# Spreading an image's prologue over the image before it, with the depthwise convolution on TensorE and per-token factors in the epilogue

## The chip, the cores and the metric

One Trainium2 chip (trn2), one core. The metric is the device time of one execution in microseconds (us), the median of several runs. Engines are named as the profile names them: PE is TensorE, PEld its weight loads, DVE is VectorE, ACT ScalarE, POOL GpSimd, SP the engine in whose queue nearly all DMAs are issued.

## The reference, cut to what matters

Four images of 48 × 48 tokens with 128 channels go through layer 0 (a group norm, a projection, a 3 × 3 depthwise convolution, a selective scan in four directions, a gated layer norm and a projection), then through attention and a spectral layer, which the change leaves alone.

```python
xz = einsum('bhwc,ec->bhwe', _gn(x), in_proj_w)          # 128 -> 2 * 256
xin, z = split(xz, 2, axis=-1)
xc = silu(depthwise_3x3(xin, conv_w) + conv_b)           # B, 256, 48, 48
xs = stack([x0, x1, x0[..., ::-1], x1[..., ::-1]])       # rows, columns, both reversed; L = 2304
# ... dt = softplus(...), B_t and C_t by projections of xs
def step(h, inp):                                        # h: B, 4, 256, 16
    dt_l, u_l, B_l, C_l = inp
    h = h * exp(dt_l[..., None] * A) + (dt_l * u_l)[..., None] * B_l[:, :, None, :]
    return h, einsum('bkdn,bkn->bkd', h, C_l)
# ... y: the four directions added, tokens by 256
y = (y - mu) * rsqrt(var + 1e-05) * norm_g + norm_b
x = x + einsum('bhwd,cd->bhwc', y * silu(z), out_proj_w)
```

## The kernel before

Each image is worked through in 20 chunks (five per direction: four of 480 tokens, one of 384). A chunk is eight *units* (two halves of the 256 channels by four groups of states). A unit makes a product with B, two scans on VectorE, a product with C on GpSimd and a sum over states on TensorE. The *prologue* (norm, projection, convolution, z) of the next image runs at the end of an image, as the first part of the preparation of its first chunk; the *epilogue* (layer norm, gate, projection) follows the last chunk.

```python
    def prologue2(b):
        # ... projection into xpad, SUB = 384 tokens at a time
            nc.vector.tensor_scalar(x, xpad[:, 0:H, 0:W], cw[:, h, 0:1], cb[:, h:h + 1], ALU.mult, ALU.add)
            for t in range(1, 9):
                yield
                dy, dx = divmod(t, 3)
                nc.vector.scalar_tensor_tensor(x, xpad[:, dy:dy + H, dx:dx + W], cw[:, h, t:t + 1], x,
                                               ALU.mult, ALU.add)
            nc.scalar.activation(x, x, AF.Silu)
        # ... z, its SiLU, and its way to DRAM
```

What every chunk sends through SP's queue: B and C (`bcd`) to DRAM early in its preparation; in the fifth unit dt and dt·u (`dtdud`) to DRAM and back, replicated (`rep`); and `fetch`, the broadcasts of rows of `bcd`, which are issued by `multiply` in the last four units of the chunk before.

```python
        def prep(self):
            # ... softplus; then for each half h:
                nc.sync.dma_start(d[h, :, :, :n].rearrange("s p t -> p s t"), re[:, h, :, :n])
                rep = rp.tile([P, 2, G4, CS], F32, tag="rep", name=f"rep{name}_{h}")
                for c in range(C4):
                    nc.sync.dma_start(rep[c * DL:(c + 1) * DL, :, :, :n],
                                      d[h, :, :, :n].rearrange("s (g p) t -> p s g t", p=DL))

        def fetch(self, i):
            t = one.tile([P, CS], F32, tag=f"bc{i}", name=f"bc{self.name}_{i}")
            for c in range(C4):
                nc.sync.dma_start(t[c * DL:(c + 1) * DL, :self.n],
                                  self.bcd[4 * i + c, :self.n].partition_broadcast(DL))

    POOLED = ((0, 3), (1, 1), (1, 3))        # units whose product with B is GpSimd's

    def multiply(s):
        u = units[s]
        u.times_c()
        # ...
        if u.h == NH - 1 and ci < len(chunks):
            chunks[ci].fetch(Q4 + u.q)
            if any(u.q == q for h, q in POOLED):
                chunks[ci].fetch(u.q)
```

The epilogue's core, with full-width factors on VectorE:

```python
        def gate(i):
            rs = rss[:, i % 2]               # 128 x 384, the same in every partition
            nc.vector.reciprocal(rs, rs)
            for h in range(NH):
                v = yf[h][:, cols(i)]
                nc.vector.scalar_tensor_tensor(v, v, ng[:, h:h + 1], rs, ALU.mult, ALU.mult)
                nc.vector.scalar_tensor_tensor(v, v, nb[:, h:h + 1], zr[i][:, h], ALU.add, ALU.mult)
```

## Time and profile before

| | before |
|---|---|
| median of 3 runs | 8763.95 us (8758.15 to 8770.22) |
| profiled execution | 8775.2 us, mean granted clock 0.799 |
| PE, DVE, ACT, POOL busy | 6433.5, 4656.9, 2975.0, 3486.1 us |
| layer 0 | to about 5059 us |
| image to image | 1265.3 us |
| last image, from its third bcd write | 1078.0 us |

The shares of busy time are averages over layer 0 (VectorE and GpSimd full, TensorE a half) and the rest (TensorE alone), so they bound nothing by themselves. The useful ruler is a mark that occurs once per chunk: the DMA that writes `bcd`. The time from one to the next is the length of a chunk, and from an image's third to the next image's third is an image. I count from the third because the writes of an image's first two chunks are mixed with the turn. The prediction below shows the lines of the page, the stretches, the groups and the queue.

### The profile page before, as it was taken

What the parts mean: (1) busy time and instruction counts of PE and PEld (TensorE: products, weight loads), DVE (VectorE), ACT (ScalarE), POOL (GpSimd) and SP (SyncE); (2) the same over time, 40 slices, a digit from 0 to 9 for tenths busy, and PEclk for the clock granted to TensorE, in tenths of its full rate; (3) what the DMA queues carried; (4) which work ended last, traced back from release to release, by engine and by line L of the source; (5) the groups of instructions that cost most, each with busy time, mean ns of one, the idle gap of its engine ahead of it and who ended that gap; (6) DMA issues with size and microseconds to landing.
All of it is one profiled execution on the core that took longest, in us unless ns stands there. A gap on an engine that the chain in (4) does not pass through costs nothing.

```text
span 8775.2 us, 62894 instructions
## 1 busy us (share of the span) xinstructions
PE 6433.5 (73%) x22344; PEld 3227.0 (37%) x22344; DVE 4656.9 (53%) x3905; ACT 2975.0 (34%) x6001; POOL 3486.1 (40%) x936
## 2 busy tenths in 40 slices
PE   4555636655545655455556589899999999999999
PEld 1111112111112111121111145466666666666666
DVE  5888858888768888668888720221111111111111
ACT  3555534555434555435555444400000000000000
POOL 3787735787736777538787600100000000000000
PEclk6666656666666666666666699999999999999999
DMA  3555514555524555425555400000000000000000
GB/s 80 117 120 119 118 49 110 115 121 121 118 57 103 116 120 119 97 65 112 118 120 120 102 25 0 6 5 11 13 8 8 8 8 14 10 8 6 6 6 22
DMA packets 377310, 570.98 MB, mean 65 GB/s; under 512 B 50073, under 2 KB 372761, under 8 KB 376994
## 3 DMA queue, kind: packets, MB, share of 16 engines
q1 hardware_dynamic: 374016, 566.19, 28.1%
q8 instruction: 175, 2.87, 0.1%
q14 instruction: 141, 1.16, 0.0%
q10 hardware_dynamic: 2978, 0.77, 0.0%
HBM read 467.68 MB, written 99.09 MB: 65 GB/s over the span
## 4 chain that ended last, share of the span: by engine, by line
PE 48%; DMA 14%; DVE 12%; issue 6%; POOL 6%; SPq 5%; ACT 3%; POOLq 0%; DVEq 0%; ACTq 0%
PE cv L780 28%; PE pr L793 6%; DMA dtdud<-re 6%; DMA rep<-dtdud 6%; DVE s L372 5%; POOL s L381 4%; PE sp L313 4%; SPq L332 4%; PE s L605 3%; PE o L611 3%; DVE xc L221 2%; DMA bc<-bcd 2%; PE y L390 2%; DVE s L357 2%; ACT dA L365 1%
## 5 line engine op out<-in xcount | busy, mean ns | idle before, releaser
L372 DVE TENSOR_TENSOR_SCAN s<-dA,s 128x962 f32<-128x962 f32 (+1 forms) x1536 | 2590.9, 1744 | 334.6 <-ACT s L369 334.5
L381 POOL TENSOR_TENSOR s<-s,bc 128x1920 f32<-128x1920 f32 (+1 forms) x640 | 2423.5, 3811 | 607.0 <-ACT carry L379 443.9
L780 PE MATMUL cv<-tt,u 128*128 128x384 f32 (+2 forms) x9216 | 2505.5, 433 | 0.0
L390 PE MATMUL y<-s,csum 128*32 128x480 f32 (+1 forms) x5120 | 923.2, 817 | 1546.1 <-POOL s L381 1544.0
L780 PEld LDWEIGHTS cv<-tt,u 128*128 128x128 f32 x9216 | 1648.5, 190 | 869.9
L365 ACT ACTIVATE dA<-rep,A 128x480 f32<-128x480 f32 (+1 forms) x2560 | 1659.2, 648 | 560.3 <-DVE s L372 515.4
L786 DVE COPY U<-cv 128x384 f32<-128x384 f32 x384 | 214.2, 558 | 2244.9 <-PE cv L780 2244.9
L357 POOL TENSOR_TENSOR s<-rep,bc 128x1920 f32<-128x1920 f32 (+1 forms) x240 | 993.6, 4140 | 930.8 <-DMA bc<-bcd 923.1
L784 ACT COPY U<-cv 128x384 f32<-128x384 f32 x384 | 183.6, 478 | 2797.3 <-PE cv L780 2797.3
L761 POOL TENSOR_TENSOR ms<-mp,mm 128x512 f32<-128x512 f32 x16 | 20.3, 1268 | 2717.5 <-DVE G L710 2439.5
L390 PEld LDWEIGHTS y<-s,csum 128*32 128x32 f32 x5120 | 128.2, 130 | 2211.5 <-POOL s L381 1959.0
L357 DVE TENSOR_TENSOR s<-rep,B 128x1920 f32<-128x1920 f32 (+1 forms) x400 | 824.0, 2060 | 35.8 <-PE B L348 17.0
L348 PE MATMUL B<-xd,spread 32*128 32x480 f32 (+1 forms) x800 | 587.1, 824 | 136.3 <-DVE s L357 123.5
L793 PE MATMUL pr<-U,G 128*128 128x288 f32 (+1 forms) x2560 | 519.2, 358 | 0.0
L793 PEld LDWEIGHTS pr<-U,G 128*128 128x128 f32 x2560 | 407.5, 190 | 67.2
L313 PE MATMUL sp<-re,ident 128*128 128x480 f32 (+1 forms) x640 | 391.0, 699 | 18.8 <-ACT re L301 12.4
L319 DVE TENSOR_TENSOR re<-sp,xc 128x480 f32<-128x480 f32 (+1 forms) x160 | 125.8, 786 | 463.8 <-ACT re L316 463.8
L796 DVE TENSOR_TENSOR acc<-acc,pr 128x288 f32<-128x288 f32 x512 | 232.5, 454 | 245.2 <-PE pr L793 245.2
L348 PEld LDWEIGHTS B<-xd,spread 32*128 32x128 f32 x800 | 161.9, 251 | 501.0 <-DVE s L357 250.5
L316 ACT COPY re<-sp 128x480 f32<-128x480 f32 (+1 forms) x160 | 86.7, 542 | 733.1 <-PE sp L313 733.1
L606 ACT ACTIVATE e<-s,shift 128x512 f32<-128x512 f32 (+1 forms) x360 | 230.6, 642 | 290.7 <-PE s L605 273.8
L611 PE MATMUL o<-e,xn 128*128 128x512 f32 (+1 forms) x720 | 293.2, 550 | 0.0
(151 smaller groups left out, 4306.8 us busy)
## 6 DMA issues: line engine op xcount, KB each, us to landing
rep<-dtdud SPq DMA_DIRECT2D x512, 480.0 KB, 8.2
bc<-bcd SPq DMA_DIRECT2D x1536, 60.0 KB, 2.1
dtdud<-re SPq DMA_DIRECT2D x128, 480.0 KB, 9.7
rep<-dtdud SPq DMA_DIRECT2D x128, 384.0 KB, 6.1
tt<-in_phi SPq DMA_DIRECT2D x32, 576.5 KB, 3.7
bc<-bcd SPq DMA_DIRECT2D x384, 48.0 KB, 2.0
dtdud<-re SPq DMA_DIRECT2D x32, 384.0 KB, 3.0
zd<-z SPq DMA_DIRECT2D x24, 384.0 KB, 2.4
```

The source lines that it names most:

```text
L313: nc.tensor.matmul(ps[:, :n], w, t, start=(i == 0), stop=(i == 3))
L332: nc.sync.dma_start(t[c * DL:(c + 1) * DL, :self.n], self.bcd[4 * i + c, :self.n].partition_broadcast(DL))
L348: nc.tensor.matmul(ps[:, :n], spread[32:64, self.q].rearrange("p c j -> p (c j)"), self.ch.xd[32:64, :n], start=True, stop=True)
L357: eng.tensor_tensor(ch.blocks(s)[:, :, ch.cols], ch.rep[self.h][:, 1, :, :n], bt[:, :n].unsqueeze(1).to_broadcast([P, G4, n]), ALU.mult)
L365: nc.scalar.activation(ch.blocks(dA[j], 2)[:, i, ch.cols], ch.rep[self.h][:, 0, g, :n], AF.Exp, scale=A[:, ch.k, self.h * G4 + g, self.q:s ...
L372: nc.vector.tensor_tensor_scan(s, dA[j][:, run], s, 0.0, ALU.mult, ALU.add)
L381: nc.gpsimd.tensor_tensor(s, s, ch.bc[Q4 + self.q][:, :n].unsqueeze(1).to_broadcast([P, G4, n]), ALU.mult)
L390: nc.tensor.matmul(ch.y[g * DL:(g + 1) * DL, :n], csum, s[:, g], start=(self.q == 0), stop=(self.q == Q4 - 1))
L605: nc.tensor.matmul(ps[:, :w], xnT[:, i * P:(i + 1) * P], xnT[:, lo:lo + w], start=True, stop=True)
L611: nc.tensor.matmul(po[q][:, :w], xn[:, i // 2, i % 2, :], e[:, lo:lo + w], start=(i == 0), stop=(i == NT - 1))
L780: nc.tensor.matmul(ps[:, lo - c0:CONV], u[b][:, J, g, :], taps(tt[q], lo - J * P - back, c0 + CONV - J * P - back), start=(J == 0), stop=( ...
L793: nc.tensor.matmul(ps[:, lo - lo0:hi - lo0], G[q][:, s, :], U[q][:, lo:hi], start=(q == 0), stop=(q == 1))
```

## The change

The intent: take the turn between images off the path. The next image's prologue becomes a list of 43 small tasks, of which a chunk takes two or three (in its units 0, 1 and 5, counted from 0; for these tasks the prediction calls unit 5 the fifth) beside its own work. The convolution becomes nine accumulating TensorE matmuls with diagonal weights, over ten rows at a time. SiLU of z moves into the epilogue. There the variance is laid out with tokens on partitions, so that its inverse root is one factor per token, applied after the projection. The convolution's result is held for two images at once, and chunks become 384 tokens long, 24 per image; I take the second to make room for the first. The core, with cuts:

```diff
-CS = 480
+CS = 384
+RB = 10
+    taps = wp.tile([P, NH, 9, P], F32, name="taps")
+    for h in range(NH):
+        for t in range(9):
+            nc.vector.tensor_scalar_mul(taps[:, h, t], ident, cw[:, h, t:t + 1])
 ...
+        def transposed(lo, n, i):
+            x = two.tile([P, 4, C], F32, tag="tok", name=f"x{b}_{i}")
+            nc.sync.dma_start(x[:m, :parts], xs[b][lo:lo + n].rearrange("(i p) c -> p i c", p=m))
+            ps = now["ps"] = mm_tile(f"tr{b}_{i}")
+            for t in range(parts):
+                nc.tensor.transpose(ps[:, t * m:(t + 1) * m], x[:m, t], ident[:m, :m])
+
+        def stats(i):
+            def pe():
+                transposed(i * SUB, SUB, f"s{i}")
+            def rest():                       # emitted one unit later
+                nc.vector.bn_stats(st[:, i], now["ps"][:, :SUB])
 ...
+                        for t in ts:          # taps 0-3 in one unit, 4-8 in the next
+                            dy, dx = divmod(t, 3)
+                            nc.tensor.matmul(out, taps[:, h, t], xpad[h][:, top + dy:top + dy + m, dx:dx + W],
+                                             start=(t == 0), stop=(t == 8))
 ...
+        def variance(i):
+            for t in range(tb):
+                for h in range(NH):
+                    nc.tensor.matmul(var[:, i * tb + t:i * tb + t + 1], sq[i][:, h, t * P:(t + 1) * P],
+                                     dmean[:, 0:1], start=(h == 0), stop=(h == NH - 1))
 ...
+        def fetch(i):
+            zr[i] = two.tile([P, NH, SUB], F32, tag="z", name=f"zr{b}_{i}")
+            nc.sync.dma_start(zr[i], zs[b][:, :, cols(i)].rearrange("h p t -> p h t"))
+            xr[i] = two.tile([P, tb, C], F32, tag="xr", name=f"xr{b}_{i}")
+            nc.sync.dma_start(xr[i], xs[b][cols(i)].rearrange("(t p) c -> p t c", p=P))
         def gate(i):
-            nc.vector.reciprocal(rs, rs)
+            nc.scalar.activation(zr[i], zr[i], AF.Silu)
 ...
+                nc.vector.scalar_tensor_tensor(xr[i][:, t], ps[:, :C], rd[:, i * tb + t:i * tb + t + 1], xr[i][:, t],
+                                               ALU.mult, ALU.add)
 ...
+        fetch(0)
+        for i in range(nblk + 1):
             if i < nblk:
-                center(i)
+                gate(i)
+            if i > 0:
+                project(i - 1)
+            if i + 1 < nblk:
+                fetch(i + 1)
 ...
+        if rest:
+            task = rest
+        elif tasks and (j == 0 or j in (1, 5) and tasks[0][0] == 1):
+            task = tasks.pop(0)
+        if task:
+            begin(task)
```

## The prediction

> **What bounds the kernel now.** I read four views in this order: the page's slices (where the stages lie), the busy time by stretches (the turn between two images against the steady part), the timeline of the DMA-issuing queue (SP), and the chain of waits. From the page:
>
> ```profile
> DVE  5888858888768888668888720221111111111111
> POOL 3787735787736777538787600100000000000000
> PEclk6666656666666666666666699999999999999999
> ```
>
> Each digit is a fortieth of 8775 us, 219 us. Layer 0, the only part that the change touches, is the first 23 slices (to about 5060 us). Attention and the spectral layer after it (3,700 us) stay as they are. In layer 0 VectorE is at 0.8, with three dips to 5 and 6: the turns from one image to the next. TensorE's granted clock is 0.6 there and 0.9 later. Two stretches show a turn against steady work:
>
> ```profile
> 800.00:1090.00 290.00, 172.94 (x540) 44.95 (x539) 247.56 (x155) 161.28 (x318) 233.40 (x62) 0.67 0.56 122
> 1090.00:1354.00 264.00, 108.83 (x284) 34.83 (x284) 163.06 (x82) 88.60 (x154) 102.34 (x24) 0.59 0.28 68
> ```
>
> The columns are TensorE, weight load, VectorE, ScalarE and GpSimd busy us, clock, DMA share, GB/s. In the turn GpSimd falls from 233 of 290 us to 102 of 264 and the DMA share halves: the scan, which feeds both, is held back. What holds it is in the groups of instructions:
>
> ```profile
> L221 DVE SCALAR_TENSOR_TENSOR xc<-xpad,cw,xc 128x2304 f32<-128x2304 f32 x64 | 213.9, 3342 | 1.8
> L429 DVE RECIPROCAL room<-room 128x384 f32<-128x384 f32 x24 | 61.1, 2546 | 0.0
> ```
>
> The first is the depthwise convolution: 8 big instructions per half image, 53 us per image (median 2.6 us, up to 6.5 when it shares time with GpSimd), queued ahead of scans. The second is the epilogue's full-width reciprocal, 15 us per image.
>
> The steady part is not bound by a full engine but by a ring of waits that closes once per chunk. The queue's timeline shows it for a chunk of 480 and then the chunk of 384 that ends each direction:
>
> ```profile
> 544.81 0.38 SPq L321 DMA_DIRECT2D dtdud<-re  x1
> 556.17 1.78 SPq L324 DMA_DIRECT2D rep<-dtdud  x4
> 558.05 2.05 SPq L332 DMA_DIRECT2D bc<-bcd  x4
> 561.45 0.30 SPq L289 DMA_DIRECT2D bcd<-xd  x1
> 563.88 12.82 SPq L332 DMA_DIRECT2D bc<-bcd  x20
> ...
> 598.93 0.38 SPq L321 DMA_DIRECT2D dtdud<-re  x1
> 606.87 1.78 SPq L324 DMA_DIRECT2D rep<-dtdud  x4
> 610.62 1.71 SPq L332 DMA_DIRECT2D bc<-bcd  x4
> 612.42 0.36 SPq L289 DMA_DIRECT2D bcd<-xd  x1
> 614.51 11.32 SPq L332 DMA_DIRECT2D bc<-bcd  x20
> 640.65 0.38 SPq L321 DMA_DIRECT2D dtdud<-re  x1
> ...
> 645.31 0.38 SPq L321 DMA_DIRECT2D dtdud<-re  x1
> ```
>
> Columns: start, time, queue and line, what is moved. The ring: dt and dt·u of the next chunk go to DRAM (L321), come back replicated (L324), then 24 row broadcasts (L332) follow in the same queue; the last of them frees GpSimd, whose product releases a scan, a sum on TensorE, the softplus matmuls, and so the next L321. **First part** (L321 to the last broadcast): 544.81 to 576.70 = 31.9 us with 480, 598.93 to 625.83 = 26.9 with 384. **Second part** (to the next L321): 576.70 to 598.93 = 22.2 with 480; 625.83 to 645.31 = 19.5 with 384. Sum: 54.1 against 46.4 us. So 0.8 of the tokens cost 0.86 of the time: 24 broadcasts have a fixed issue cost. The two 384-chunks that follow one another in the middle of an image confirm it: L289 to L289 is 45.8 us there.
>
> **What the Trainium skill says.** *TensorE: Matmul & The Clock Gate*, Part 1, says that the array runs at half clock after an idle window of about 3.4 us and at full clock after a busy one. The trace agrees: the same eight sums (L390) take 1.83 us after an idle stretch and 1.01 us in a dense one. So convolution matmuls of 480 columns are 0.40 us per pass warm and 0.80 cold (spacing of the weight loads of L313, two passes per matmul). *ScalarE: Activation LUTs*, What ACT_TABLE_LOAD costs, gives 1283 ns per switch of the function set plus a drain; the trace has 1283 ns each (L168, L223, L425). *Perfetto Trace Analysis*, DMA Instruction — HWDGE, says that the profiled window of a DMA instruction leaves out the data movement; the trace agrees (L321 shows 0.38 us, its reader starts 11 us later), so I took gaps in the queue, not durations.
>
> **The change part by part.**
>
> *Size of the turn before.* The third bcd write of image 0 is at 184.9 us, of image 1 at 1450.5: a period of 1265.7 us. The 17 intervals from 184.9 to 1085.4 average 53.0, so 20 chunks are 1060 us and the turn costs 206 us: the epilogue's 55 (1356 to 1411) and 150 of prologue.
>
> *Removed from VectorE:* 8 × 2.6 and 1.5 us, twice per image, with contention 56 us, plus group-norm scaling of 1.5 us. Removed too: ScalarE waiting for it, and the serial ip and z matmuls (each ~8 us).
>
> *Moved to TensorE:* 10 convolutions (5 blocks of rows by 2 halves) of 18 instructions per image, 18 × 0.4 = 7.3 us warm, up to 14.5 cold; 73 to 145 us per image. They are issued in the first two units of a chunk, where TensorE waits 16 to 17 us per chunk for GpSimd (L390 at 586.73 sat 16.1 us idle). They mostly fit, and may warm the array for the sums after them. Hence the 150 us should leave the path.
>
> *Cost of spreading, per image.* 43 tasks in 18 of the chunks. Ten z writes and three token loads fall in the queue's critical part (fifth unit): about 1.5 us each for issue and transfer. Transposes waiting for their tokens at the head of TensorE's queue: 3 × 4 us in that slot. The SiLU with two table loads, 2 × 2.1 + 2 × 1.3 = 6.8 us on ScalarE, mostly exposed. Sum about 37 us; less about 1.2 us for each of 10 chunks with a warm array: 25 us.
>
> *Chunks of 384:* 24 × 46.4 = 1114 us instead of 1060: +54 per image.
>
> *Epilogue.* Gone: reciprocal 15 us, one of two scalar_tensor_tensor (7.8 us), sqrt over full width. Added: the variance as 72 instructions with one column (weight-load bound), and 180 projection instructions instead of 72. L441 issues 14 in 3.37 us, 0.24 each; if warm, 0.15 to 0.19 (otr L630: 18 in 2.6). So projection 27 to 43 us, variance 11 to 17, mean 24 × 0.4 = 10, table loads, filling and draining about 10: 68 us, bound by TensorE instead of VectorE, against 55.
>
> *New period:* 1114 + 68 + 5 (flush, start of y) + 25 = 1212, against 1266: −54, three times = −161. The last image has no next one: +54 body, +13 epilogue. *Start:* the first prologue is now all serial: statistics to about 22 us as before, then 5 blocks of about 22 us (20 of TensorE work, 2 of gaps; the last shorter) = 110, SiLU 7, preparation 31: first scan input at 170 instead of 135.7: +34 us.
>
> **Sum:** −161 + 54 + 13 + 34 = −60; 8764 − 60 = **8704**, say 8705 us.
>
> **Rivals.**
> 1. *The turn vanishes almost freely and the ring gets shorter:* warm TensorE cuts sums and softplus matmuls in every chunk, the epilogue overlaps the queue's 27 us wait. For it: the idle 16 us; VectorE is only 81% needed in a 46 us chunk (37.4 us of work, estimated from 16 scans of 1.66, 5 products of 1.65 and four small ones). Then spreading costs 0 and the epilogue 50: about −190 us, 8575. Against it: in the ring's first part VectorE is busy without a gap, so postponed scans are not free.
> 2. *The spread work lengthens the ring:* evacuations, z writes and transposes that wait for DMA sit in in-order queues, and two PSUM buffers are shared by B, dt, softplus and tasks. For it: the ring has only 2.4 us of slack at VectorE (scan at 583.08). With 3 us in each of 18 chunks, or a cold convolution spilling over the softplus matmuls: spreading 55 to 80, total +30 to +105, about 8830.
> 3. *The turn was hidden anyway.* Against it: GpSimd and DMA halve there, so no.
> 4. *Smaller chunks cost nothing* (24 × 44): −115 more. Against it: the measured 45.8 to 46.4.
>
> **Range and chances.** Spreading 0 to 60 us (times three), epilogue 50 to 85 (times four), start +20 to +90 (cold array): about ±100 us together. 8600 to 8810. Faster by 2% needs 175 us, nearly all of rival 1: 0.16. Slower by 2% needs rival 2 and a cold start: 0.04. Within 2%: 0.80.
>
> **What would show it.** L289 to L289 at 46 to 48 us in chunks with tasks, 46.4 in the last six; no dip of GpSimd at a turn beyond some 75 us; period about 1212; first scan near 170 us; TensorE busy in layer 0 up, its clock somewhat higher; epilogue with TensorE as the dense engine. The prediction is wrong if 384-chunks without tasks differ from 46.4, if chunks with a convolution are over 50 us, or if the epilogue is over 90.

## The result, and the profile after

The changed kernel is correct and took **8839.38 us** (median of 4 runs, 8826.48 to 8843.20) against 8764.69 in the same rounds. The ratio is 1.0083, 95% interval 1.0065 to 1.0100: within 2%, as given the largest chance, but slower where 60 us less was predicted, and outside the range. A ratio here and below is the mean time of one kernel's fast runs over the mean of the other's of the same rounds, so not quite the ratio of the medians quoted.

The slices of the page after, in the same form as those of before; a slice is now 221 us:

```profile
DVE  1777776777876778767788621131111111111111
POOL 1677774677765777757777600000000000000000
PEclk8677767677776777676666689999999999999999
```

VectorE's dips to 5 at the turns are gone, and TensorE's clock in layer 0 is mostly 0.7 instead of 0.6. But the flat level is 7, where it was 8 between the turns. TensorE is busy for 6937.9 us instead of 6433.5 and VectorE for 4390.1 instead of 4656.9. So the work moved as intended, and the plateau between the turns lost what the turns gained. The first slice has fallen from 5 to 1: the start is longer.

The chunks, measured from `bcd` write to `bcd` write:

| | predicted | measured |
|---|---|---|
| image to image (third bcd write to third bcd write) | 1212 | 1243 (1245.3, 1242.1, 1241.3) |
| the first three chunks that carry tasks, per image | | 55.9, 61.5, 57.8 (mean 58.3) |
| the next 15 with tasks | 46 to 48 | 48.2 |
| the last five of the image | 46.4 | 47.1 |
| chunks of the last image, no tasks | 46.4 | 46.9 |
| across the turn, with one chunk in it | 46.4 + 68 + 5 | 111 |
| third bcd write of image 0 | 219 (185 + 34) | 233.3 |

Three stretches, in the columns that the prediction explained: one of the first three chunks with its neighbour's start, one later chunk with tasks, one chunk without:

```profile
284.00:350.00 66.00, 30.99 (x105) 10.72 (x105) 47.30 (x33) 25.28 (x56) 39.18 (x14) 0.60 0.39 89
455.00:504.00 49.00, 38.20 (x127) 12.74 (x119) 38.80 (x26) 27.69 (x57) 36.95 (x12) 0.74 0.50 114
4010.00:4056.00 46.00, 26.67 (x98) 8.57 (x96) 35.47 (x24) 25.30 (x58) 34.24 (x11) 0.65 0.46 108
```

The second stretch has 11.5 us more TensorE work than the third, and such a chunk is only 1.3 us longer (48.2 against 46.9): matmuls between the waits cost little. In the first, TensorE does least for its length (31 of 66 us) and its clock is lowest: it is not overfull but waiting. SP's queue shows for what:

```profile
286.69 1.78 SPq L411 DMA_DIRECT2D bc<-bcd  x4
289.25 0.30 SPq L368 DMA_DIRECT2D bcd<-xd  x1
291.00 0.39 SPq L204 DMA_DIRECT2D x_s<-in_x  x1
293.06 19.18 SPq L411 DMA_DIRECT2D bc<-bcd  x20
```

The load of the tokens for the statistics (`x_s`) is issued at 291.00, behind the replication and the broadcasts, because SP issues in order and stood at the replication's wait for `dtdud`. TensorE, at the same time:

```profile
277.68 0.85 PE L469 MATMUL y<-s,csum 128*32 128x384 f32 x8 [0.24 <-POOL s L460]
296.38 0.88 PE L207 MATMUL tr_s<-ident,x_s 128*128 128x128 f32 x3 [17.85 <-DMA x_s<-in_x]
```

The bracket is the idle time before the instruction and what ended it. TensorE finished its sums at 278.5, came to the transposes that stand next in its queue and sat idle for 17.85 us. VectorE follows:

```profile
297.30 0.56 DVE L214 BATCH_NORM_STATS2 gst<-tr_s 128x6 f32<-128x384 f32 x1 [13.13 <-PE tr_s L207]
...
317.45 3.09 DVE L226 SCALAR_TENSOR_TENSOR gg<-gg,gmv 128x1 f32<-128x1 f32 x1
```

The statistics instruction was emitted a unit later, and by then was to be free; instead it held the scans behind it for 13.13 us. Summed over layer 0, the waits that go back to the tokens, and one of the epilogue (engine, line, what was waited for; total us, times, longest us; other lines of the view left out):

```profile
PE tr L207 <- DMA x<-in_x: 207.5, 19, 17.3
ACT xT L247 <- PE tr L207: 198.7, 19, 15.9
PE tr_s L207 <- DMA x_s<-in_x: 143.8, 13, 18.0
DVE gst L214 <- PE tr_s L207: 88.5, 12, 13.1
ACT zr L524 <- DMA zr<-zd: 71.5, 16, 5.3
```

TensorE waits 351 us for tokens. Part of it falls in the serial start, and part in time in which TensorE has nothing else to do; which part costs is for the experiments. The last line is of the epilogue.

The later chunks show it too, outside the fifth unit. Every third of the 15 (four per image) carries the load of a block's tokens in its first unit. One such load is issued at 661.43, behind 20 broadcasts and a write of z, and TensorE sat 11.3 us until 664.53. These four average 50.2 us, the other eleven 47.4.

Line 226 above is a side finding: an instruction on 128 × 1 elements took 3.09 us, and in the serial start of image 0 such ones take 0.16 to 0.22. GpSimd's line for the same moment:

```profile
317.36 6.29 POOL L460 TENSOR_TENSOR s<-s,bc 128x1536 f32<-128x1536 f32 x2
```

Two products of some 3.14 us; the first ends at 320.5, VectorE's tiny one at 320.54. The Trainium skill, *SBUF — State Buffer*, "Who interferes with whom", says that a VectorE instruction with two SBUF inputs contends with a GpSimd instruction that reads SBUF, that the shared ports are an exclusive lock, and that the order of issue decides who blocks. The trace agrees: the two other tiny instructions of this kind (L225, L235) took 2.93 and 3.38 us and also ended with GpSimd's. Images 1 to 3 pay it three times each, some 9 us in one chunk of VectorE; what that costs in time no run isolates.

The epilogue, in the chain that ended last (start, duration, what):

```profile
2648.56 0.85 ACT zr L524
...
2650.77 1.22 PE op L534 x4
...
2653.61 0.36 DVE xr L540
2653.99 0.36 SPq L542
...
2654.45 3.37 DMA zr<-zd
...
2663.82 3.26 DMA zr<-zd
```

A block of the second half takes 9.4 us (2654.45 to 2663.82). TensorE is busy for 5.7 of them, but its projections are only about 2.5 us of the chain. The rest is one loop: z is fetched (3.4), its SiLU, the product, TensorE, the last add; then SP issues the write of the result (L542), which waited for that add, and only behind it the next fetch of z. The first half, the mean and the variance (2617.7 to 2635.2), is TensorE's: it is busy for 16.9 of these 17.5 us.

### The profile page after: what moved, and what is told of

It reads as the page before. It is cut to its first block, busy times and chain, and to the rows that moved or that the text cites. A ratio compares the mean times of both kernels' runs of the same rounds, so it can differ in the third digit from the quotient of the medians.

```text
span 8836.9 us, 71496 instructions
## 1 busy us (share of the span) xinstructions
PE 6937.9 (79%) x25300; PEld 3608.8 (41%) x25300; DVE 4390.1 (50%) x3967; ACT 3179.2 (36%) x7043; POOL 3480.6 (39%) x1129
## 4 chain that ended last, share of the span: by engine, by line
PE 51%; DMA 18%; DVE 10%; SPq 7%; issue 7%; POOL 4%; ACT 3%; POOLq 0%; ACTq 0%; DVEq 0%
PE cv L895 28%; DMA dtdud<-re 7%; DMA rep<-dtdud 7%; PE pr L908 6%; SPq L411 5%; DVE s L451 5%; PE sp L392 4%; POOL s L460 4%; PE s L720 3%; PE o L726 3%; DVE s L436 2%; DMA bc<-bcd 2%; PE y L469 2%; SPq L403 1%; PE cv L281 1%
## 5 line engine op out<-in xcount | busy, mean ns | idle before, releaser
L451 DVE TENSOR_TENSOR_SCAN s<-dA,s 128x770 f32<-128x770 f32 x1536 | 2607.5, 1744 | 408.7 <-ACT s L448 407.0
L460 POOL TENSOR_TENSOR s<-s,bc 128x1536 f32<-128x1536 f32 x768 | 2423.0, 3178 | 469.5 <-ACT carry L458 451.1
L444 ACT ACTIVATE dA<-rep,A 128x384 f32<-128x384 f32 x3072 | 1794.2, 584 | 469.8 <-DVE s L451 416.6
L469 PE MATMUL y<-s,csum 128*32 128x384 f32 x6144 | 930.4, 696 | 1081.0 <-POOL s L460 1079.9
L436 POOL TENSOR_TENSOR s<-rep,bc 128x1536 f32<-128x1536 f32 x288 | 993.0, 3448 | 1044.2 <-DMA bc<-bcd 971.7
L436 DVE TENSOR_TENSOR s<-rep,B 128x1536 f32<-128x1536 f32 x480 | 834.9, 1739 | 123.6 <-PE B L427 65.9
L427 PE MATMUL B<-xd,spread 32*128 32x384 f32 x960 | 607.1, 722 | 127.6 <-DVE s L436 106.2
L392 PE MATMUL sp<-re,ident 128*128 128x384 f32 x768 | 408.2, 619 | 21.3 <-ACT xpad L264 16.8
L398 DVE TENSOR_TENSOR re<-sp,xc 128x384 f32<-128x384 f32 x192 | 129.5, 674 | 532.4 <-ACT re L395 532.4
L281 PE MATMUL cv<-xpad,taps 128*128 128x480 f32 (+1 forms) x720 | 340.8, 626 | 0.1
```

The lines of the kernel that those rows point to most:

```text
L281: nc.tensor.matmul(out, taps[:, h, t], xpad[h][:, top + dy:top + dy + m, dx:dx + W], start=(t == 0), stop=(t == 8))
L392: nc.tensor.matmul(ps[:, :n], w, t, start=(i == 0), stop=(i == 3))
L427: nc.tensor.matmul(ps[:, :n], spread[32:64, self.q].rearrange("p c j -> p (c j)"), self.ch.xd[32:64, :n], start=True, stop=True)
L436: eng.tensor_tensor(ch.blocks(s)[:, :, ch.cols], ch.rep[self.h][:, 1, :, :n], bt[:, :n].unsqueeze(1).to_broadcast([P, G4, n]), ALU.mult)
L444: nc.scalar.activation(ch.blocks(dA[j], 2)[:, i, ch.cols], ch.rep[self.h][:, 0, g, :n], AF.Exp, scale=A[:, ch.k, self.h * G4 + g, self.q:s ...
L451: nc.vector.tensor_tensor_scan(s, dA[j][:, run], s, 0.0, ALU.mult, ALU.add)
```

## The experiments

**Theory A**: the loss is in the token loads. Each stands behind another DMA's wait in SP's queue, and TensorE, VectorE and ScalarE, which take their work in order, wait for it in turn. **Theory B**: the convolution's matmuls lengthen the ring. **Theory C**: the 384-token chunk was mis-sized. **Theory D**: the epilogue, through its fetches.

All results, each against the kernel before in the same rounds:

| run | median us | ratio (95%) |
|---|---|---|
| changed kernel | 8839.38 | 1.0083 (1.0065 to 1.0100) |
| e1_loads_act | 8779.60 | 1.0011 (0.9996 to 1.0026) |
| e2_loads_ahead | 8709.71 | 0.9931 (0.9917 to 0.9946) |
| e3_before_384 | 8978.66 | 1.0241 (1.0225 to 1.0256) |
| e4_conv_one_tap | 8831.98 | 1.0071 (1.0054 to 1.0088) |
| e5_one_bc | 9065.25 | 1.0339 (1.0322 to 1.0357) |
| e6_before_one_bc | 9058.41 | 1.0332 (1.0317 to 1.0348) |
| e7_epi3 | 8752.01 | 0.9984 (0.9969 to 0.9999) |
| e8_all | 8855.81 | 1.0101 (1.0086 to 1.0116) |
| e9_order | 8387.04 | 0.9567 (0.9553 to 0.9582) |
| e10_ahead_epi | 8617.71 | 0.9832 (0.9817 to 0.9846) |
| e11_ahead_epi_order | 8061.77 | 0.9197 (0.9182 to 0.9213) |
| e12_before_order | 8350.55 | 0.9528 (0.9514 to 0.9542) |

All are correct except e4, which is wrong. Differences to the changed kernel are taken across rounds, some on other chips; the kernel before moved by less than 4 us between them (8764.69 to 8768.24).

### Which part lost it: e1 to e4

**e1_loads_act**, on the changed kernel, takes the token loads out of SP's queue and leaves everything else:

```diff
-            nc.sync.dma_start(x[:m, :parts], xs[b][lo:lo + n].rearrange(...))
+            nc.scalar.dma_start(x[:m, :parts], xs[b][lo:lo + n].rearrange(...))
```

> The changed kernel with its token loads issued from ScalarE's queue instead of SP's; nothing else differs. Theory A (the token load of a task in the fifth unit stands in SP's queue behind the dt round trip, and the transposes and statistics that need it block TensorE and VectorE): the first three chunks of images 0 to 2, now 55.9, 61.5 and 57.8 us apart, fall to 48 to 51, and the time from 8839 to 8730 to 8770 us. Rival B (the added convolution matmuls lengthen the ring): no change beyond 15 us. Rival C (the small group-norm operations of VectorE waiting for GpSimd are what costs): third chunk stays near 58, the first two too.

Measured: 8779.60, so 60 us less, a little short of the expected range. The first three chunks fell from a mean of 58.3 us to 49.3, the third of them to 47, so it was not the small group-norm operations (rival C); the later ones stayed at 48.2. So Theory A holds for the first three. Nine such chunks in three images would give 81 us. Of the other 20 some 16 were lost again around the turns (117.9 and 116.5 us across the first two, where the changed kernel has 111.0 and 110.3) and 4 in the last image; why, no run shows. TensorE still waits 114 us for tokens in e1 (68.7 and 45.1); that ScalarE, busy with the exponentials, issues the loads late is likely, but was not tested.

**e2_loads_ahead** keeps SP's queue and issues each load one task earlier, so that its wait lies behind it when TensorE comes:

```diff
+        todo = [(i * SUB, SUB, f"s{i}", 3) for i in range(L // SUB)]
+        # ... and the blocks; load() pops one, issues it and appends the tile to loaded
+        load()
         def transposed(lo, n, i):
-            x = two.tile([P, 4, C], F32, tag="tok", name=f"x{b}_{i}")
-            nc.sync.dma_start(x[:m, :parts], xs[b][lo:lo + n].rearrange(...))
+            load()
+            x = loaded.pop(0)
```

> The changed kernel with each token load issued one load ahead of its use, on the same SP queue: same traffic, no wait at the head of TensorE's queue. Theory A: as the run with ScalarE's queue or better, 8690 to 8750 us, with the transposes of tasks no longer idle-waiting on the load (143.8 + 207.5 us of TensorE waiting in the changed kernel, to under 60). If traffic on the queue and not the wait were the cause, this run would stay near 8839 while the run with ScalarE's queue gains.

Measured: 8709.71, so 130 us less than the changed kernel and 0.7% less than the kernel before. The waits that answer to those above:

```profile
PE tr_s L221 <- DMA x_s<-in_x: 52.6, 11, 13.2
DVE gst L228 <- PE tr_s L221: 16.7, 6, 6.1
DVE gg L249 <- POOL gg L248: 34.6, 4, 12.3
```

TensorE's wait for the blocks' tokens (207.5 us before) is gone from the list. The first three chunks take a mean of 49.1 us and the others 47.5; the four with a block's load fell from 50.2 to 47.9. Of the first three the second still takes 53.1: the third line is its cause as far as the trace shows, VectorE waiting 11 to 12 us per image for a tiny power operation of GpSimd's (L248). Of the 130 us, some 83 are the nine chunks ((58.3 − 49.1) × 9), 26 the start (first scan input at 161.2 instead of 187.0 us, since there the loads stood behind the z writes), the rest the later chunks. The changed kernel was 75 us behind the kernel before, so **Theory A accounts for more than all of that difference.**

**e3_before_384**, on the kernel before, tests Theory C:

```diff
-CS = 480
+CS = 384
```

> The kernel before with chunks of 384 alone. The ring with 384 measures 46.4 to 46.9 us per chunk, so 24 x 46.9 = 1126 instead of 1060 us per image, four times: 8764 + 264 = 9030 us, say 9000 to 9050. Rival (a chunk costs in proportion to its tokens): 8764 plus or minus 30.

Measured: 8978.66, so 211 us more than before. The prediction's term was 4 × 54 = 216, so by the total Theory C falls. By the chunk it does not: a chunk of e3 takes 46.9 us in all four images, as my expectation had it, and 24 × 46.9 less the 20 × 52.9 of before is 68 us per image instead of 54. The total hides it, since the turn of e3 is 20 us shorter than before (188 against 208 us beyond its chunks) and its third bcd write 16 us earlier. The smaller chunk alone costs 2.4%, so the rest of the change must have won back most of it.

**e4_conv_one_tap**, on the changed kernel: in images 1 to 3 only the middle one of nine taps, so 8/9 of the convolution's matmuls are gone (relative error 0.50).

```diff
+                            if b == 0 or t == 4:
-                            nc.tensor.matmul(out, taps[:, h, t], ..., start=(t == 0), stop=(t == 8))
+                                nc.tensor.matmul(out, taps[:, h, t], ...,
+                                                 start=(b > 0 or t == 0), stop=(b > 0 or t == 8))
```

> The changed kernel with one tap instead of nine in the spread convolutions of images 1 to 3 (wrong result on purpose; image 0 unchanged): 480 matmul instructions fewer. Theory: the convolution lies in TensorE's idle time, so the time stays within 15 us of 8839. Rival B (the convolution lengthens the ring by 1.5 us in each of 10 chunks of three images): 8794 or less.

Measured: 8831.98, 7 us less, inside the spread of the runs. Theory B falls: the convolution on TensorE is hidden. This is a net effect: the mean clock fell from 0.822 to 0.810 without these matmuls, so the run doesn't separate their own time from what they do to the clock.

### The epilogue: e7 and e10

**e7_epi3**, on the changed kernel: three buffers for the z and x blocks, fetched two ahead; the squares, which die before, share z's buffers (that edit and the one for x are left out here).

```diff
-            zr[i] = two.tile([P, NH, SUB], F32, tag="z", name=f"zr{b}_{i}")
+            zr[i] = three.tile([P, NH, SUB], F32, tag="z", name=f"zr{b}_{i}")
         fetch(0)
+        fetch(1)
 ...
-            if i + 1 < nblk:
-                fetch(i + 1)
+            if i + 2 < nblk:
+                fetch(i + 2)
```

> The changed kernel with three buffers for z and x blocks in the epilogue and both fetched two blocks ahead (the squares share the z buffers). Theory: the projection half of the epilogue waits for the z fetch (71.5 us of ScalarE waits in 16 places), 9.3 us per block instead of about 6; the epilogue falls from 68 to 50 to 55 us, four times: 8839 to 8770 to 8800. Rival (my prediction: TensorE binds the epilogue): within 15 us of 8839.

Measured: 8752.01, so 87 us less, more than expected. The gap across a turn fell from 111 to 88 us; four epilogues of 22 us are 88. ScalarE's wait for z, 71.5 us before:

```profile
ACT zr L524 <- DMA zr<-zd: 4.7, 7, 1.6
```

So the second half of the epilogue was bound by its fetches, as Theory D has it. Whether the third buffer does it or the fetch's earlier place in SP's queue, this run doesn't separate. It is no part of the miss, since its length was predicted rightly, but a second thing to mend. **e10_ahead_epi** has both repairs:

> The changed kernel with token loads one load ahead and three epilogue buffers. The two causes lie in different stretches (the first chunks, the turn), so the gains add: 8839 - 130 - 87 = 8622 us, 8605 to 8640. If they shared a wait the sum would be short by 30 us or more.

Measured: 8617.71. The two gains add up (8839 − 130 − 87 = 8622): they are separate waits.

### An attempt at the ring that failed: e5, e6, e8

Every row set needs four broadcasts. The prediction blamed the fixed issue cost of 24 DMAs for the smaller chunk's price. **e5_one_bc** (on the changed kernel) and **e6_before_one_bc** (on the kernel before) make them one:

```diff
-            for c in range(C4):
-                nc.sync.dma_start(t[c * DL:(c + 1) * DL, :self.n],
-                                  self.bcd[4 * i + c, :self.n].partition_broadcast(DL))
+            src = self.bcd[4 * i:4 * i + 4, :self.n]
+            row = list(src.ap)
+            nc.sync.dma_start(t[:, :self.n], bass.AP(src.tensor, src.offset, [row[0], [0, DL], row[1]]))
```

> The changed kernel with each group of four row broadcasts (L411) as one DMA: 6 issues per chunk instead of 24, same bytes. Theory (the steady ring is bound by SP's queue: fixed issue cost of 24 broadcasts, some 0.6 us each): the last 20 broadcasts take about 6 us instead of 12, a chunk without tasks 40 to 43 us instead of 46.9, and the time falls by 96 chunks x 4 to 6 us, to 8250 to 8500 us. Rival (the bytes in flight bind, not the issues): chunks stay at 46 to 47, 8800 or more.

> The kernel before with the same edit. Theory: a chunk of 480 falls from 53.0 to 47 to 50 us, 80 chunks, 8764 to 8380 to 8550 us; less gain than with chunks of 384, since there are fewer issues. Rival: no change.

Both were misses: 9065.25 and 9058.41, over 3% slower. A chunk of e5 without tasks takes 49.3 us instead of 46.9, and the 17 chunks from an image's third bcd write on (of both lengths) average 56.5 us in e6 instead of 52.9. A stretch of e5 in which only these broadcasts move:

```profile
4640.00:4643.00 3.00, 0.00 (x0) 0.00 (x0) 3.00 (x2) 1.04 (x2) 0.00 (x0) 0.50 0.27 95
```

The last two columns are the mean share of the 16 DMA engines and GB/s: 0.27 of 16 is some four engines. The Trainium skill, *DMA: Bandwidth & Descriptors*, "Rules for kernel authors", says that a slowest dimension of fewer than 16 confines a DMA to as many engines. The source pattern here starts with a dimension of 4, and the trace agrees. So fewer issues were bought with a quarter of the engines. That this is what makes the chunk longer is argued, not shown: in a like stretch of the changed kernel (4630 to 4634) the share is 0.38 to 0.41, but the rate only 105 to 107 GB/s against 95. Nothing follows from these runs on what an issue costs. **e8_all** joined e2, e5 and e7 before that was clear:

> Token loads one load ahead, one broadcast DMA per group, and three epilogue buffers together. If the three causes are independent the gains add: 8839 - 130 (token loads, measured) - 55 (epilogue) - 450 (broadcasts) = about 8200, say 8080 to 8350 us. If the ring then binds on GpSimd or VectorE (34 and 37 us of work per chunk) the gain is smaller: 8350 to 8450.

Measured: 8855.81, a miss of some 500 us. Against e10, which is the same without the single broadcast, that is 238 us more.

### What the ring waits for: e9, e12, and all together in e11

In a chunk without tasks GpSimd's first product with B still waits for a broadcast. That set of rows (`bc3`) is issued last of the six, behind sets for the products with C, which are needed later. **e9_order** (on the changed kernel) and **e12_before_order** (on the kernel before) issue the same DMAs in the order of need:

```diff
-            chunks[ci].fetch(Q4 + u.q)
-            if any(u.q == q for h, q in POOLED):
-                chunks[ci].fetch(u.q)
+            for i in ((4, 1), (3, 5), (6,), (7,))[u.q]:
+                chunks[ci].fetch(i)
```

> The changed kernel with the broadcasts of a chunk in another order on the same queue: the two groups of B rows that free GpSimd's first product are issued with the first C group instead of last; same DMAs. Theory (the ring closes through the last broadcast, 10.7 us of GpSimd waiting per chunk): GpSimd starts its first product up to 8 us earlier, a chunk without tasks takes 40 to 43 us instead of 46.9, the time falls to 8300 to 8550 us. Rival (the ring is held by VectorE, which is busy through that stretch): chunks fall by under 2 us, 8650 or more.

> The kernel before with the new broadcast order alone. Theory: a chunk of 480 falls from 53.0 to 47 to 50 us, 8764 to 8380 to 8550 us, so that the order explains no difference between the two kernels but bounds both. Rival: 8700 or more.

Measured: 8387.04 and 8350.55, the second a little below its range. GpSimd's wait for broadcasts, in the changed kernel over 950 us of the last image and in e9 over 580 us of it:

```profile
POOL s L436 <- DMA bc<-bcd: 216.4, 20, 12.5
```

```profile
POOL s L436 <- DMA bc<-bcd: 62.6, 12, 5.6
```

Per wait that is 10.8 us against 5.2, and a chunk went from 46.9 to about 41 us: the chunk shortened by what the wait lost. In e12 the mean of the same 17 chunks per image went from 52.9 to 47.3 us. e9's queue in a chunk:

```profile
4211.47 7.89 SPq L411 DMA_DIRECT2D bc<-bcd  x8
4219.45 0.37 SPq L368 DMA_DIRECT2D bcd<-xd  x1
4219.87 7.38 SPq L411 DMA_DIRECT2D bc<-bcd  x16
```

The same 24 issues, but no longer one tail of 20 at whose end the next product stood. This fault is in both kernels, so it explains nothing of the difference between them. But it means that the change can be judged with it removed: **e11_ahead_epi_order** has all three repairs.

> All three edits: token loads ahead, three epilogue buffers, broadcast order. If the order theory holds, 8622 - 96 x 4 to 6 us = 8050 to 8240 us; if not, 8560 to 8622.

Measured: **8061.77 us** (8059.45 to 8064.32), ratio 0.9197: it beats both kernels, and e12 by 289 us. With the order mended on both sides, the change as it came is slower (8387 against 8351), and with its loads and fetches mended 3.5% faster. In the shorter ring the token loads cost more: in e9 the chunks with a block's load take 50.1 us and the others of the 15 some 40.6.

## Why the prediction was wrong

By its own steps:

1. *The path of before is a ring that ends with the last broadcast, and the turn comes on top*: right. e9 and e12 cut the ring at that place and gained 5.5 to 6 us per chunk.
2. *The convolution mostly fits into TensorE's idle time*: right (e4, 7 us for 8/9 of it in three images). The turn did lie on the path and has left it, against rival 3; the dips are gone.
3. *Chunks of 384 cost +54 per image*: too small by some 12 us per image (24 × 0.5). A chunk without tasks takes 46.9 instead of 46.4 in the changed kernel, and so it does in e3: the half microsecond comes with the chunk's length and not with the tasks. The 46.4 was one chunk of before. That e3 as a whole met 216 (211) was luck, since its shorter turn made up for it.
4. *Cost of spreading, 25 us per image*: **this step failed**. Measured are 3 × (58.3 − 46.9) = 34 us in the first three chunks and 15 × (48.2 − 46.9) = 19 in the others, 53 in all. The term of the sum is "Transposes waiting for their tokens at the head of TensorE's queue: 3 × 4 us in that slot". The slot, the number of loads and the kind of wait were right; the size was about 9 us each instead of 4 (58.3 − 49.1, what e2 took away; with the rest of these chunks' excess 11.4), because the wait isn't a transfer alone. It is the transfer plus SP's place behind the `dtdud` round trip (17.85 us of idle TensorE at 296.38), and it is passed on through VectorE or ScalarE, which hold scans or exponentials behind it. The prediction took the fifth unit for critical in the queue and yet charged the load as if it were free to start. For the four block loads outside this slot it charged no wait; they cost some 3 us each (50.2 against 47.4), 11 of the 19. Its own terms add up to 38.3 and not to 37, which matters little. It was rival 2 that came true, through the loads and not through the convolution that it also named.
5. *Epilogue 68 us, bound by TensorE*: 68 us measured (2617.7 to 2685.6). TensorE binds the mean and the variance (17.5 us, predicted 21 to 27), but the 50 us of the projection are bound by its fetches (e7). A right number for a reason that was wrong in the larger part, so in part luck. The turn as a whole was 111 us instead of the 120 that the sum has, as part of a chunk overlaps it.
6. *Start, first scan at 170 us*: 187 measured. The array was warm (slice 1 at 0.8), so the named risk was not it; the token loads behind the z writes were (26 us in e2).

The miss of 134 us as a sum: start 14; spreading 3 × 28 = 84; the half microsecond per chunk 3 × 12 = 36; the turns 3 × −9 = −27; the last image 14, mostly again that half microsecond; and 13 because the profiled executions differ by less (61.7 us) than the medians (74.7).

The range failed in a way of its own. Spreading (53, given 0 to 60), epilogue (68, given 50 to 85) and start (+51 for the scan, given +20 to +90) all lay inside their ranges. But spreading and start erred to the same side, both through the same queue, and the length of a chunk, which is multiplied by 96, had been given no range. The range was also narrower than its own terms: around the 8704 they give −75 to +105, −72 to +68 and −14 to +56, which combined as independent errors (root of the squares) is −105 to +137, up to 8841. "About ±100" cut the upper side.

What stays open: why a chunk of 384 among its like takes 46.9 us and one among chunks of 480 45.8 to 46.4, why e1 lost 16 us at the turns, and the 0.8 us by which a later chunk with tasks is longer even in e2 (47.5 against 46.7).

## What to carry to other kernels

Work that is moved into a stage's idle time brings its loads into that stage's DMA queue: look up where in the in-order queue each load will stand, and issue it one step before the engine asks for it, since an engine that waits for it stops everything behind it. Order the DMAs of a queue by when their readers need them: here that alone was worth over 4% in both kernels. Before merging small DMAs into one, look at its outermost dimension.

## What the Trainium skill lacked or had wrong

- *DMA: Bandwidth & Descriptors*, "Issuing engines are not separate DMA queues", says that issuing on several engines saves only the issue time, which is usually small. Here 11 token loads per image moved to another issuing engine gained 60 us (8839 to 8780), and issued one step earlier in the same queue 130 us, since the queue holds a load behind another DMA's wait: TensorE stood up to 18.0 us. The section doesn't mention this.
- *ScalarE: Activation LUTs*, "What ACT_TABLE_LOAD costs", has 1283 ns and a drain of some 1380 ns per switch. The trace of the changed kernel has the 1.28 us (loads at 2633.50 and 2635.19), but the instructions behind them start at 2634.90 and 2636.49, hardly 0.1 us after the loads' ends, and the loads begin 0.01 us after the ends of the instructions before them (2633.49 and 2635.18): no drain is to be seen there.
- *FP8 and Floating Point Precision*, "TensorE Precision Notes", says that true fp32 takes four passes through the array, but not in how many instructions a profile shows them. In the trace of before an fp32 matmul of 480 columns (L313) shows as two, 0.40 us apart warm and 0.80 us cold.
- *SBUF — State Buffer*, "Who interferes with whom", is right on the shared ports, but doesn't warn of the smallest instructions, which lose most in proportion: one on 128 × 1 elements took 3.09 us beside GpSimd's products and such ones 0.16 to 0.22 us without them.
